# x1's transposes moved from TensorE to VectorE and DMA in a graph-attention kernel, with more rooms for u and the sums of x

## The chip, the cores and the metric

The kernel runs on one core of a Trainium2 chip. The core has a matrix engine (TensorE, PE in the profile; PEld is its weight load), VectorE (DVE), ScalarE (ACT), GpSimd (POOL), and SyncE (SP), which here only issues DMAs; 16 DMA engines move data between HBM and on-chip memory. Each engine works through its own instructions in the order in which the program gives them, and waits on semaphores for what it needs from others. The metric is the device time of one execution in microseconds, the median of several runs.

## The reference

There are 4096 nodes with 512 features each, and a matrix adj of 4096 x 4096. All is float32. Layer 0 is attention with adj as bias, then a residual and a layer norm; layer 1 is two graph convolutions, again with residual and norm:

```python
# layer 0
q = x @ Wq.T + bq;  k = x @ Wk.T + bk;  v = x @ Wv.T + bv
a = q @ k.T / sqrt(512) + adj + adj
x1 = layernorm(x + softmax(a, axis=-1) @ v)
# layer 1
h = relu(adj @ (x1 @ W1) + b1)          # W1: 512 x 128
out = layernorm(x1 + adj @ (h @ W2) + b2)
```

## The kernel before

**Groups and passes.** The 4096 query rows are cut into 8 groups of 512 (g = 0 to 7), and each group into 4 row tiles of 128 (r = 0 to 3). Scores are formed transposed: keys on the partitions, queries along the free dimension. q and k are never made. M = Wq.T Wk is formed first, and u = M.T xT for each group (half scale, plus a bias); the scores of group g are then xT.T u_g + adj.T. A pass over a group is 16 units of 7 gaps, 112 gaps, and each gap holds two score products of 256 columns. Softmax divides at the end: the maximum over keys is kept in macc, exp is taken by ACT, the row sums are kept in lacc, and p = x.T s is accumulated (so that v = x Wv.T is applied once per group, to p, by `rows_out_fast` or `rows_out`).

**Winograd's form of Strassen.** Most products are of 2 x 2 blocks with seven products in place of eight. A step k in ORDER = (1, 2, 6, 7, 5, 4, 3) multiplies one operand of the left side by one of the right side; operands are quarters (such as B11, B21, B22, B12) or sums of quarters (S1 to S4 on the left, T1 to T4 on the right). Its results accumulate in two PSUM banks, X and Y, that are read out after each step by DVE or ACT, so the bank must have been read before the step after next can use it. Each float32 product shows in the profile as two matmul records; a transpose by PE shows as one.

**What a gap holds besides scores.** A list `work` gives each stretch of units items with an estimated PE time, which are dealt out evenly among its gaps: in the pass of group g these are the 224 px items of group g - 1 (0.43 us each by the kernel's own estimate, `PX_US`), with the row items of group g - 2 put between them by `row_items`; `w(n)` stands for the next n px items. In the last pass, that of the px items of group 7, there are no scores, and w(n) is 3n items. px is done in phases: block of key pairs by step k. Phase n starts by asking for the x tile of phase n + 3 (`load_x`). `hooks`, filled by `at(unit, place, f)`, tell at which gap loads, sums and softmax steps are issued.

**First pass.** In the pass of group 0 there is no px yet. Its items are u of the later groups: u of groups 0 and 1 by `u_products` (16 products of 512 columns; group 0 before the first score), u of groups 2 to 7 by `u_fast` (28 products of 256 columns). u goes to HBM (`store_u`, POOL's queue) and is loaded again as the right operand of its group (`load_operand`). In the same pass x is loaded in pairs of tiles (`sum_x(q)`, into one of three rooms in t_sb, which is otherwise empty until x1's product with W1), read by DVE for a constant (`row_parts`), summed by POOL and stored as the left operands of px (xs_d). The left operands S1 to S4 of the scores are formed by DVE and stored too (`form_s`, `store_s`), and xT is loaded in two rotating tiles (`load_xts`).

**Rows.** `rows_out_fast` (groups 0 to 5, named by FAST_V) multiplies p by Wv in seven steps and adds the rest in XR; `rows_out` (groups 6 and 7) does it in 16 products of 512. Then, for each of the four row tiles, the norm is applied by ACT (`rows_norm`), PE transposes the tile in four 128 x 128 blocks into PSUM and ACT copies it out (`project`, lines 736 to 743), PE multiplies by W1 (`project2`, into t_sb), and POOL adds b2 and stores x1 for the last residual (`add_b2`). The order is in the list of `row_items`: the norms of row tiles 2, 3, 0 and 1 are followed within a few px items by their transposes. XR has one room (pool `rows`), so the rows of group g + 1 can be loaded only when those of g are done with. The same pool has one room with the tag "x1t", for a transposed tile and for the sum s3 of `rows_out_fast`.

**After attention.** The graph convolutions follow (`strassen`, lines 1041 and 1342), with the rows of group 7 among their first products. They are not touched.

Of the kernel before, what the change touches and what calls it, by code (L numbers as in the profile page):

```python
# [18 lines left out]
P = 128  # L19
# [5 lines left out]
def tile_graph_attention_then_gcn(  # L25
# [80 lines left out]
    c_d = [dram.tile([1, W], F32, name=f"c_d{g}") for g in range(NG)]  # L106
    u_d = [dram.tile([P, 7, 2, HW], F32, name=f"u_d{g}") for g in range(NG)]
# [46 lines left out]
    FAST_V = range(NG - 2)  # L154
# [10 lines left out]
    def new_uo(b, what):  # L165

        u = UO.setdefault(b, {})
        if what in (B11, B12):
            u[what] = uop.tile([P, 2, HW], F32, tag="b1", name=f"b1_{b}_{what}", bufs=3)
        else:  # L170
            u["all"] = uop.tile([P, 5, 2, HW], F32, tag="ut", name=f"uo{b}")
            u.update({k: u["all"][:, k - 1] for k in range(1, 6)})

    def store_u(b, what):
        if what in (B11, T4):
            nc.gpsimd.dma_start(u_d[b][:, what], UO[b][what])
        else:
            nc.gpsimd.dma_start(u_d[b][:, 1:6], UO[b]["all"])

    def m_sums():  # L180
# [6 lines left out]
        for out_, a, b_ in ((T1, T3, B11), (T2, B22, T1), (T4, B21, T2)):  # L187
            nc.gpsimd.tensor_tensor(MV[out_], MV[a], MV[b_], ALU.subtract)

    def m_t3():  # L190

        nc.vector.tensor_tensor(MV[T3], MV[B22], MV[T3], ALU.subtract)

    def u_fast(b):
# [4 lines left out]
        def read(k):  # L199
            ps = X["X" if k in (1, 6, 5, 3) else "Y"].rearrange("p (o i) -> p o i", o=2)  # L200
            if k == 1:
                new_uo(b, B11)
            if k == 6:
                new_uo(b, B12)
            if k == 7:
                new_uo(b, "all")
# [10 lines left out]
            if k == 4:  # L217
                for out_, a, b_ in ((T1, B12, B11), (T2, B22, T1), (T3, B22, B12)):
                    nc.gpsimd.tensor_tensor(u[out_], u[a], u[b_], ALU.subtract)
                store_u(b, B11)  # L220
            if k == 3:
                store_u(b, "all")
                owing.append(lambda: last(b))

        def last(b):
            nc.vector.tensor_tensor(UO[b][T4], UO[b][B21], UO[b][T2], ALU.subtract)
            store_u(b, T4)
# [25 lines left out]

    def u_products(b):

        ps = {}

        def one(o, c):
            def go():
                if c == 0:  # L260
                    ps[o] = bank("o", f"psu{b}_{o}", 4)
                nc.tensor.matmul(  # L262
                    ps[o], m_t[:, c, ts(o, P)], XTS[b][:, c, :], start=c == 0, stop=c == ND - 1
                )
                if c == ND - 1:
                    if o == 0:
                        if b:
                            for what in (B11, B12, "all"):
                                new_uo(b, what)
                        else:  # L270
                            for k in ORDER:
                                new_operand(0, k)
                    pair = (B11, B12) if o < 2 else (B21, B22)
                    for h in range(2):
                        nc.scalar.activation(
                            (UO[b][pair[h]] if b else UT[0, pair[h]])[:, o % 2, :],
                            ps[o][:, ts(h, HW)],
                            AF.Identity,
                            bias=ub_t[:, o : o + 1],
                            scale=HALF_SCALE,  # L280
                        )
                    if o == ND - 1:
                        if b:
                            combine_u(nc.gpsimd, UO[b])
                            for what in (B11, "all", T4):
                                store_u(b, what)
                        else:
                            combine_u(nc.vector, {k: UT[0, k] for k in range(7)})

            return go  # L290

        return [one(o, c) for o in range(ND) for c in range(ND)]

    def combine_u(eng, ut):
        for out_, a, b_ in ((T1, B12, B11), (T2, B22, T1), (T3, B22, B12), (T4, B21, T2)):
            eng.tensor_tensor(ut[out_], ut[a], ut[b_], ALU.subtract)
# [52 lines left out]
    def sum_x(q):  # L349

        w = t_sb[:, ts(q % 3, 8), :].rearrange("p (a b) c -> p a (b c)", a=4)
# [307 lines left out]
    def rows_out_fast(g, k, j):  # L659
# [6 lines left out]

        def read(k):
# [22 lines left out]
        if (k, j) == (1, 0):  # L690
            read_px()
            T["s3"] = rowp.tile([P, 2, HW], F32, tag="x1t", name=f"s3_{g}")
            tt(T["s3"], a11, a21, ALU.subtract)
            tt(a21, a21, a22, ALU.add)
# [17 lines left out]
        if j == 0 and n:  # L712
            read(ORDER[n - 1])
            if k == 2:
                tt(a11, a21, a11, ALU.subtract)
            if k == 6:
                tt(a12, a12, a11, ALU.subtract)
# [18 lines left out]
    def project(g, r):  # L736
# [6 lines left out]
        T["x1t", g, r] = x1t  # L743

# [9 lines left out]
    def row_items(g, between):  # L754
# [21 lines left out]
        w = between  # L776
        if g in FAST_V:
            return [
                *(item(0.86, rows_out_fast, g, k, j) for k in ORDER for j in range(2)),
                *w(1), item(0, rows_last, g), *norm(2), *norm(3), *w(2), *pro(2), *w(2), *pro(3),  # L780
# [12 lines left out]
    with tc.tile_pool(name="wqk", bufs=1) as wp:  # L793
# [47 lines left out]
        for w_t, w_n, name, b_t, b_r in (  # L841
            (wq_t, wq_n, "bk", bk_t, bk_r), (wk_t, wk_n, "bq", bq_t, bq_r)
        ):
            in_every_row(name, b_t, b_r)
            for o in range(ND):
                ps = bank("o", f"psw{o}", 4)
                for c in range(ND):
# [23 lines left out]
    for f in first[:ND]:  # L871
        f()
# [524 lines left out]
```

## Time and profile before

| | |
|---|---|
| median of three runs | 2306.16 us (2304.3 to 2306.61) |
| the profiled execution | 2308.84 us, span 2307.1 us |
| TensorE busy | 2276.3 us, 99% |
| VectorE busy | 1617.0 us, 70% |
| GpSimd busy | 1018.7 us, 44% |
| ScalarE busy | 399.8 us, 17% |
| DMA | 525.14 MB, mean 228 GB/s |

The span is the time from the first to the last instruction of the profiled execution; the 1.7 us between it and that execution's time lie around it. A line of the timeline reads: start, duration, engine, line of the kernel, operation, out<-in, tile shape, count, and in brackets the idle time before it with what ended it. A line of the waits reads: who waited, for whom, in total, how often, the longest. Busy time of matmuls includes a pipelined tail, so their price is read from start to start. Stages by time: M and u of group 0 until 39.5 us, the first pass until about 250, seven passes of 210 to 214 us (a group's rows begin at 442.13, 656.18, 870.58, 1084.5, 1298.95 and 1512.91 us), the pass without scores from 1718 to 1853, the graph convolutions to the end.

### The profile page before, as it was taken

The numbers are of one execution on the slowest core, as the hardware profiler recorded it, in microseconds if no ns is written. First come the engines' busy times: TensorE is split into PE (matmuls) and PEld (weight loads), VectorE is DVE, ScalarE is ACT, GpSimd is POOL, SyncE is SP. The second block draws the span as 40 slices with busy tenths as digits, with TensorE's granted clock in tenths as the row PEclk, the third lists the DMA queues.
The fourth block names the chain that finished last, engine by engine and source line by source line (L and its number), as shares of the span: only waits on it lengthen the run. The fifth ranks groups of instructions, "written<-read, shape, count | busy, mean of one in ns | idle before, by whom it ended". The sixth has DMA issues, their size and how long they took to land.

```text
span 2307.1 us, 28475 instructions
## 1 busy us (share of the span) xinstructions
PE 2276.3 (99%) x10672; PEld 1750.6 (76%) x10672; DVE 1617.0 (70%) x2276; ACT 399.8 (17%) x438; POOL 1018.7 (44%) x1009
## 2 busy tenths in 40 slices
PE   9999999999999999999999999999999999999998
PEld 5888788888888888888888888888876743333456
DVE  4676776687667756765776687568657877888864
ACT  2212211131122112111311121122102000000012
POOL 3565654185327424731653274237429830001043
PEclk9999999999999999999999999999999999999999
DMA  6999878667857684777578586947754468899996
GB/s 177 273 284 309 233 215 230 193 174 215 246 135 218 189 246 114 215 213 215 151 221 232 145 218 193 259 117 210 196 191 155 155 237 321 332 347 375 352 383 218
DMA packets 282711, 525.14 MB, mean 228 GB/s; under 512 B 23184, under 2 KB 130448, under 8 KB 281680
## 3 DMA queue, kind: packets, MB, share of 16 engines
q1 hardware_dynamic: 229040, 406.12, 52.3%
q0 software_dynamic: 43296, 105.39, 20.7%
q10 hardware_dynamic: 10240, 11.82, 1.7%
q8 instruction: 85, 1.39, 0.2%
q14 instruction: 50, 0.41, 0.0%
HBM read 475.27 MB, written 46.41 MB: 226 GB/s over the span
## 4 chain that ended last, share of the span: by engine, by line
PE 92%; DVE 4%; POOL 2%; DMA 1%; issue 1%; ACT 0%; SPq 0%; POOLq 0%; DVEq 0%; ACTq 0%
PE p L576 32%; PE X L436 18%; PE b L1041 15%; PE Y L436 14%; PE v L703 3%; PE acce L1342 2%; PE psu L234 2%; PE ops L1296 1%; PE tps L749 1%; PE psu L262 1%; PE x L651 1%; PE x1ps L740 1%; DVE s L449 1%; PE psm L856 1%; DMA u_d<-uo 1%
## 5 line engine op out<-in xcount | busy, mean ns | idle before, releaser
L576 PE MATMUL p<-s,xn 128*128 128x256 f32 x3584 | 895.6, 380 | 7.0 <-DVE s L531 2.6
L576 PEld LDWEIGHTS p<-s,xn 128*128 128x128 f32 x3584 | 677.1, 190 | 111.0 <-DVE s L531 5.6
L436 PE MATMUL X<-ut,sa 128*128 128x256 f32 x1984 | 513.4, 381 | 1.7 <-DVE s L449 1.7
L492 POOL TENSOR_TENSOR lacc<-lacc,s 128x512 f32<-128x512 f32 x240 | 344.1, 1434 | 203.2 <-ACT s L483 192.3
L436 PEld LDWEIGHTS X<-ut,sa 128*128 128x128 f32 x1984 | 370.1, 190 | 64.2 <-DVE s L449 15.3
L449 DVE TENSOR_TENSOR s<-X,s 128x512 f32<-128x512 f32 x256 | 176.3, 689 | 278.6 <-PE X L436 278.2
L436 PE MATMUL Y<-ut,sa 128*128 128x256 f32 x1408 | 361.6, 380 | 0.2 <-DVE s L449 0.2
L436 PEld LDWEIGHTS Y<-ut,sa 128*128 128x128 f32 x1408 | 266.8, 190 | 37.7 <-issue 1.4
L483 ACT ACTIVATE s<-s 128x1024 f32<-128x1024 f32 x128 | 135.3, 1057 | 790.3 <-DVE s L479 790.3
L458 DVE TENSOR_TENSOR macc<-macc,s 128x512 f32<-128x512 f32 x240 | 258.1, 1075 | 1.2
L449 DVE TENSOR_TENSOR s<-Y,s 128x512 f32<-128x512 f32 x192 | 131.9, 687 | 157.0 <-PE Y L436 155.7
L479 DVE TENSOR_TENSOR s<-s,mb 128x512 f32<-128x512 f32 x256 | 231.2, 913 | 2.4 <-ACT mb L399 2.4
L385 POOL DMA_DIRECT2D s<-in_adjT_dram x64 | 84.4, 1318 | 256.7 <-ACT s L380 255.9
L549 DVE TENSOR_TENSOR ot<-p,ot 128x512 f32<-128x512 f32 x248 | 168.9, 681 | 31.4 <-PE p L576 31.2
L1008 DVE TENSOR_TENSOR tt<-ck 128x1024 f32<-128x1024 f32 x112 | 138.4, 1270 | 38.7 <-PE b L1041 33.6
L1041 PE MATMUL b<-tt,st 128*64 128x512 f32 (+1 forms) x768 | 156.0, 541 | 0.0
L380 ACT COPY s<-cb 128x2048 f32<-128x2048 f32 x64 | 121.0, 1890 | 48.1 <-PE p L576 39.8
L519 POOL TENSOR_TENSOR s<-s 128x256 f32<-128x256 f32 x128 | 124.6, 974 | 0.6
L1041 PEld LDWEIGHTS b<-tt,st 128*64 128x64 f32 x768 | 53.9, 137 | 87.8 <-issue 79.9
L526 DVE TENSOR_TENSOR s<-s 128x512 f32<-128x512 f32 x128 | 114.3, 914 | 0.0
L520 POOL TENSOR_TENSOR s<-s 128x256 f32<-128x256 f32 x128 | 107.8, 842 | 10.0
L489 POOL TENSOR_TENSOR lacc<-s 128x512 f32<-128x512 f32 x8 | 10.6, 1321 | 197.9 <-ACT s L483 197.9
(186 smaller groups left out, 2112.6 us busy)
## 6 DMA issues: line engine op xcount, KB each, us to landing
ck<-in_adjT_dram SPq DMA_DIRECT2D x128, 1024.0 KB, 7.4
s<-in_adjT_dram POOLq DMA_DIRECT2D x64, 1024.0 KB, 11.5
sa<-s_d SPq DMA_DIRECT2D x224, 256.0 KB, 5.7
xn<-in_x_dram SPq DMA_DIRECT2D x192, 256.0 KB, 4.3
xn<-xs_d SPq DMA_DIRECT2D x96, 512.0 KB, 5.7
sa<-in_xT_dram SPq DMA_DIRECT2D x168, 256.0 KB, 4.7
xn<-xs_d SPq DMA_DIRECT2D x64, 256.0 KB, 3.9
ut<-u_d SPq DMA_DIRECT2D x49, 256.0 KB, 7.2
```

What stands on the lines that cost most here:

```text
L380: nc.scalar.copy(s, CB[g].unsqueeze(1).to_broadcast([P, 4, W]))
L436: nc.tensor.matmul(T["X" if k in (1, 6, 5, 3) else "Y"][:, ts(j, HW)], SA[g, d, a][:, c, j, :], UT[g, b][:, c, :], start=k in (1, 2, 7) an ...
L449: nc.vector.tensor_tensor(ck, ps, ck, ALU.add)
L458: nc.vector.tensor_tensor(MACC[g], MACC[g], ck[:, h, :], ALU.max)
L479: nc.vector.tensor_tensor(ck, ck, MB[g], ALU.subtract)
L483: nc.scalar.activation(ck, ck, AF.Exp, scale=2.0)
L492: nc.gpsimd.tensor_tensor(LACC[g], LACC[g], ck[:, h, :], ALU.add)
L519: nc.gpsimd.tensor_tensor(b12, b12, b11, ALU.subtract)
L549: nc.vector.tensor_tensor(to, ps, to, ALU.add)
L576: nc.tensor.matmul(T["PX" if k in (1, 6, 5, 3) else "PY"][:, ts(f, HW)], XN[n][:, q - a, ts(f, P)], quarters(g, q)[{1: 0, 2: 2, 6: 1, 7: 0 ...
L1008: nc.vector.tensor_tensor(t[:, :2], v[:, :, 1], v[:, 0], ALU.subtract)
L1041: nc.tensor.matmul(BK[n][k][ts(half, HH)], lhs, right(u, i, half, b), start=q == 0, stop=q == NP - 1,)
```

## The change

*x1's transposes.* For groups 0 to 5 the four row tiles are no longer transposed by PE. `turn_blocks` has DVE transpose a tile in blocks of 32 x 32 in one instruction, into the x1t tile. `store_blocks` has SP write it to HBM with four DMAs, one for each 32 partitions, in such places that the blocks come to lie transposed as well (runs of 32 words). `load_blocks` has SP load it back, over the row tile in XR, and `project2` multiplies from there. The list of `row_items` puts 70 px items after the last norm, then add_b2 of a tile, its transpose, its store 5 items later, the next tile's transpose and the load 16 items after the transpose, and the product 14 to 16 items after the load. Group 6 keeps PE's transposes, but its rows now go through `rows_out_fast`, with four of the sums on POOL instead of DVE.

*u.* `u_products` is gone: u of all groups comes from `u_fast`, which for group 0 writes into the operand tiles directly. M's sums for it are made before the first pass, and the products of M, the transposes of Wk and the constants are interleaved anew there. B21 gets a tile of its own and ACT's queue for its store, and the other tile (now four slices) is stored one step earlier. The work of the first pass starts at unit 1 in place of 0 and 3.

*Sums of x.* They have five rooms in place of three (two in the x tiles of px, which are idle then), and are loaded two units ahead in place of one. S1 to S4 are stored six gaps later.

```diff
-    FAST_V = range(NG - 2)
+    FAST_V = range(NG - 1)
...
-        if what in (B11, B12):
-            u[what] = uop.tile([P, 2, HW], F32, tag="b1", name=f"b1_{b}_{what}", bufs=3)
+        if what in (B11, B12, B21):
+            u[what] = uop.tile([P, 2, HW], F32, tag="b1", name=f"b1_{b}_{what}", bufs=4)
         else:
-            u["all"] = uop.tile([P, 5, 2, HW], F32, tag="ut", name=f"uo{b}")
+            u["all"] = uop.tile([P, 4, 2, HW], F32, tag="ut", name=f"uo{b}")
...
     def store_u(b, what):
-        if what in (B11, T4):
+        if what == B21:
+            nc.scalar.dma_start(u_d[b][:, what], UO[b][what])
+        elif what in (B11, T4):
             nc.gpsimd.dma_start(u_d[b][:, what], UO[b][what])
         else:
-            nc.gpsimd.dma_start(u_d[b][:, 1:6], UO[b]["all"])
+            nc.gpsimd.dma_start(u_d[b][:, 2:6], UO[b]["all"])
...
             if k == 4:
                 for out_, a, b_ in ((T1, B12, B11), (T2, B22, T1), (T3, B22, B12)):
-                    nc.gpsimd.tensor_tensor(u[out_], u[a], u[b_], ALU.subtract)
-                store_u(b, B11)
+                    (nc.gpsimd if b else nc.vector).tensor_tensor(
+                        u[out_], u[a], u[b_], ALU.subtract
+                    )
+                if b:
+                    store_u(b, B11)
+                    store_u(b, "all")
             if k == 3:
-                store_u(b, "all")
+                if b:
+                    store_u(b, B21)
                 owing.append(lambda: last(b))
...
-    def u_products(b):
...
     def sum_x(q):
 
-        w = t_sb[:, ts(q % 3, 8), :].rearrange("p (a b) c -> p a (b c)", a=4)
+        if q % 5 < 3:
+            w = t_sb[:, ts(q % 5, 8), :].rearrange("p (a b) c -> p a (b c)", a=4)
+        else:
+            w = xnp.tile([P, 4, 2 * P], F32, tag="xn", name=f"w{q}")
...
+        sum_ = (nc.gpsimd if g == NG - 2 else nc.vector).tensor_tensor
...
-            tt(T["s3"], a11, a21, ALU.subtract)
-            tt(a21, a21, a22, ALU.add)
+            sum_(T["s3"], a11, a21, ALU.subtract)
+            sum_(a21, a21, a22, ALU.add)
...
             if k == 2:
-                tt(a11, a21, a11, ALU.subtract)
+                sum_(a11, a21, a11, ALU.subtract)
             if k == 6:
-                tt(a12, a12, a11, ALU.subtract)
+                sum_(a12, a12, a11, ALU.subtract)
...
+    def turn_blocks(g, r):
+        T["x1t", g, r] = rowp.tile([P, ND, P], F32, tag="x1t", name=f"x1t{g}_{r}")
+        nc.vector.transpose(T["x1t", g, r].rearrange("p c i -> p (c i)"), XR[g][:, r, :])
+
+    def store_blocks(g, r):
+        x1t = T.pop(("x1t", g, r))
+        to = xt_d[g, r].rearrange("(b i) c (a j) -> a i c b j", i=32, j=32)
+        for a in range(4):
+            nc.sync.dma_start(
+                to[a], x1t[ts(a, 32)].rearrange("i c (b j) -> i c b j", j=32)
+            )
+
+    def load_blocks(g, r):
+        T["x1t", g, r] = XR[g][:, r, :].rearrange("p (c i) -> p c i", i=P)
+        nc.sync.dma_start(T["x1t", g, r], xt_d[g, r])
...
+        if g < NG - 2:
+            turn, store, load = (
+                lambda r, f=f: [item(0, f, g, r)] for f in (turn_blocks, store_blocks, load_blocks)
+            )
+            return [
+                *(item(0.86, rows_out_fast, g, k, j) for k in ORDER for j in range(2)),
+                *w(1), item(0, rows_last, g), *norm(2), *norm(3), *w(8), *norm(0), *w(2), *norm(1), *w(70),
+                *b2(2), *w(3), *turn(2), *w(5), *store(2), *b2(3), *w(11), *turn(3), *load(2), *w(5),
+                *store(3), *b2(0), *w(11), *turn(0), *load(3), *pro2(2), *w(5), *store(0), *b2(1),
+                *w(11), *turn(1), *load(0), *pro2(3), *w(5), *store(1), *w(11), *load(1), *pro2(0),
+                *w(14), *pro2(1),
+            ]
         if g in FAST_V:
...
-                *w(1), item(0, rows_last, g), *norm(2), *norm(3), *w(2), *pro(2), *w(2), *pro(3),
+                *w(1), item(0, rows_last, g), *norm(2), *norm(3), *w(2 + 2 * (g == NG - 2)), *pro(2), *w(2),
+                *pro(3),
...
-    work[0] = 3, [(0.86, f) for f in u_products(1)]
-    work[3] = 13, [(0.86, f) for g in range(2, NG) for f in u_fast(g)] + [(0, lambda: owing.pop()())] * 2
-    at(1, 0, m_sums)
-    at(3, 0, m_t3)
+    work[1] = 15, [(0.86, f) for g in range(1, NG) for f in u_fast(g)] + [(0, lambda: owing.pop()())] * 2
...
-        at(2 * d, 1, store_s, d)
+        at(2 * d + 1, 0, store_s, d)
     for q in range(NP):
-        at(max(q - 1, 0), 0, sum_x, q)
+        at(max(q - 2, 0), 0, sum_x, q)
```

## The prediction

> **What bounds the kernel now.** I read the page first, for busy time and the chain.
>
> ```profile
> span 2307.1 us, 28475 instructions
> ...
> PE 2276.3 (99%) x10672; PEld 1750.6 (76%) x10672; DVE 1617.0 (70%) x2276; ACT 399.8 (17%) x438; POOL 1018.7 (44%) x1009
> ...
> PE 92%; DVE 4%; POOL 2%; DMA 1%; issue 1%; ACT 0%; SPq 0%; POOLq 0%; DVEq 0%; ACTq 0%
> ```
>
> TensorE (PE) works 2276.3 of 2307.1 us: 31 us of idle in all. So time falls in two ways, by taking work from PE or by removing one of its few waits, and it rises wherever another engine is made late. The timeline of PE then gives the true price of a matmul, start to next start (busy times include a pipelined tail).
>
> ```profile
> 29.21 10.47 PE L262 MATMUL psu<-xt,m_t 128*128 128x512 f32 x24
> 39.52 1.03 PE L436 MATMUL X<-ut,xt 128*128 128x256 f32 x4
> ```
> ```profile
> 455.78 1.03 PE L703 MATMUL v<-wvs_t,ot 128*128 128x256 f32 x4
> 456.65 1.03 PE L436 MATMUL Y<-ut,sa 128*128 128x256 f32 x4
> ...
> 465.41 0.65 PE L740 MATMUL x1ps<-ident,xr 128*128 128x128 f32 x4 [0.40 <-ACT xr L639]
> ...
> 467.63 0.60 PE L740 MATMUL x1ps<-ident,xr 128*128 128x128 f32 x4
> 468.07 1.03 PE L436 MATMUL X<-ut,sa 128*128 128x256 f32 x4
> ```
>
> One 512-wide record takes 10.31 / 24 = 0.43 us (two records are one product), a 256-wide one 0.87 / 4 = 0.216, and the four transposes of a row tile 468.07 - 467.63 = 0.44. The third line also shows PE waiting 0.40 us for a norm. The waits of PE, whole run, name the rest:
>
> ```profile
> PE X L436 <- DVE s L449: 4.1, 5, 1.0
> ...
> PE x1ps L740 <- ACT xr L639: 2.3, 6, 0.4
> ...
> PE psu L234 <- ACT uo L211: 1.9, 1, 1.9
> ```
>
> The first and last fall between 40 and 260 us, the pass in which u and the sums of x are made. The waits of VectorE (DVE), ScalarE (ACT) and SyncE's queue (SP) in those 220 us say who is behind them; the windows show what the 1.9 us did to the clock (the last columns are PEclk, DMA share, GB/s).
>
> ```profile
> DVE t_sb L408 <- DMA t_sb<-in_x_dram: 9.7, 5, 5.0
> ```
> ```profile
> ACT uo L211 <- DMA u_d<-uo: 16.8, 3, 6.0
> ```
> ```profile
> SPq L353 <- DMA xs_d<-t_sb: 71.5, 9, 11.3
> ```
> ```profile
> 145.00:150.00 5.00, 5.00 (x17) 4.11 (x16) 2.55 (x5) 0.00 (x0) 0.95 (x1) 0.67 0.95 168
> ```
>
> Loads of x stand on SP until a room is stored; a u tile can't be written until its predecessor is stored.
>
> **The change part by part.**
>
> *1. Transposes leave PE.* 6 groups x 4 rows x 0.44 = **10.6 us** of PE, all on the bounding engine. The six waits of L740 for the norm (2.3 us) go too, since nothing on PE follows the norm until 70 items later: **2.3**. ACT loses 24 copies (L742) of 0.59 us; it is 17% busy, so that is worth nothing.
>
> *2. Seven half products for four whole ones.* u of groups 0 and 1 and the rows of group 6 go from 16 products of 512 (32 x 0.43 = 13.75) to 28 of 256 (56 x 0.216 = 12.1): 1.65 each. For u, **3.3**. For group 6 the stage (1718 to 1792 us) holds 7.5 us of PE waits, most of them on DVE and POOL: PE may arrive sooner and wait. DVE gets seven additions of 0.69 for four of 0.74 (+1.9 us); POOL gets four sums at 1.27 (+5.1), but idles 27 us just before 1724, and trades 12 small norm operations for 8. Between -3 and +3 us; I keep **1.6**, PE's own saving.
>
> *3. Rooms.* u: its slices other than B21 are stored one product earlier and B21 has its own tile, so ACT's 16.8 us of waiting and PE's 1.9 us should end, with the throttled clock behind it: 5 us at 0.67 is 1.7 us. Together 3.6. x: a sum's load stood at unit q-1 behind an xT load that waits for PE, so some were released 0.3 unit (3.5 us) before their use, against a landing of 8.1; at q-2, with five rooms, 1.3 units (15 us). Of DVE's 4.1 us brought onto PE I take 2. Against this, storing S is moved six gaps later, in three groups behind an xT load that PE releases, about 10 us before its room is wanted again; and the first adjacency load is now issued after a POOL sum, which waits on DVE, and has less time to land: after M's last product come an eviction and T2 on DVE (0.2 + 0.7 + 0.7), T4 on POOL (1.3) and the issue (1.3), 4.2 us, against 12.1 of u and 1.7 of scores until the first read, so 9.6 us where 11.5 is the median landing. I charge 1.6. Sum **4.0**, bounds -2 (both new waits, old ones stay) and +8.5 (all 6.8 of that pass and the clock). The prologue otherwise fills a 0.49 us wait for wk with other products: within that 1.6.
>
> On the clock the trace differs from the Trainium skill. "TensorE: Matmul & The Clock Gate", Part 1, has the clock halved after an idle window of about 3.4 us, so a 1.9 us wait would cost itself alone; the row shows 0.67 after it. By the page the sum would be 1.7 us smaller.
>
> *4. What is added.* Per row DVE transposes one 128x512 tile, SP issues four stores in runs of 128 bytes (2048 pieces) and one load of 256 KB, and PE multiplies from the loaded tile. No transpose or such store is in this trace.
>
> DVE: between 0.69 us (128x512 subtraction, L693) and 1.34 (the slowest such, L328), 24 times. In the stretch of the second px pass where they come:
>
> ```profile
> sum 52.00, PE 52.00 PEld 45.29 DVE 37.87 ACT 8.86 POOL 22.44; mean PE 13.00 PEld 11.32 DVE 9.47 ACT 2.22 POOL 5.61
> ```
>
> DVE is free 3.5 us of every 13, the spacing of the transposes: covered; without that cover it would be 17 to 32 us.
>
> The wait: the tile has one room, so transposes 2, 3 and 4 of a group stand on DVE until the stores before them have landed, with all score additions queued behind. A pass of 112 gaps takes 214 us, 1.9 per gap; 16 items of 0.43 (a gap takes 1.0) are 6.9 gaps, 13 us; the store comes 5 items, 4 us, after its transpose. That leaves **9 us**. Past that, the next score read may be one k-step (two gaps, 3.7 us) late before PE lacks a bank, so PE feels a landing over **12.7 us**. The nearest rows:
>
> ```profile
> x_d<-xb POOLq DMA_DIRECT2D x32, 256.0 KB, 4.0
> ...
> cb<-c_d ACTq DMA_DIRECT2D x7, 256.0 KB, 5.9
> ...
> c_d<-c_sb ACTq DMA_DIRECT2D x7, 2.0 KB, 9.8
> ```
> ```profile
> q10 hardware_dynamic: 528, 0.00, 0.5%
> ```
>
> Low: 4.0, the same bytes in 2 KB rows. High: c_d, 512 pieces, lands 3.9 us after cb; four times the pieces make 15.6, on 4.0: 20 us, 7 too many, 18 times, **130 us lost**. The last line (740 to 800 us, ACT's queue alone) gives 0.5% of 16 x 60 us for 528 packets, 9 ns each: the pieces hardly load the engines, so four DMAs side by side should take little longer than one. I take c_d's 9.8 and 1 us more, 11 us: DVE 2 us late, inside its cover. I charge **1.0** for coincidences with tight px steps.
>
> A page speaks against this. "VectorE: DVE Perf Modes", The three transpose paths, warns that a strided DMA copy as a transpose is 19 times slower than the crossbar (1309 ns per 128x128 block), when the innermost destination stride is large: estimated 25 us a block, 100 a row, and by that over 1500 us lost. Here the innermost run is 32 contiguous words, so I don't apply it. "DMA: Bandwidth & Descriptors", Specifications, puts line rate at 512 bytes and up; no row here shows 128.
>
> SP: the four issues take some 0.45 us each. The load stands 9 us after the stores, so SP stands 2 us at 11. Loads behind it: sa are issued 10 gaps (19 us) ahead and land in 5.7; xn three phases of 8 items (20 us) ahead, 5.7. Some 13 us are spare. The load itself has 13 us to its product, landing 4 to 6. POOL's adds of b2 and their stores are spread, none is added. ACT issues seven stores of B21, 0.4 us each, beside idle.
>
> **Sum.** 10.6 + 2.3 + 3.3 + 1.6 + 4.0 - 1.0 = 20.8. The profiled execution took 2308.84 us (span 2307.1 and 1.7 around it): 2288.0 after. It lies 2.7 above the median of the three runs, 2306.16, so I forecast **2286** for the median.
>
> **The rivals.**
>
> *A. The first pass and group 6 give nothing.* DMA share is about 1.0 from 150 to 250 us, so more rooms may only lengthen the queue. For: 317 to 320 GB/s there, with DMA share 0.99 to 1.02. Against: the 9.7 us of DVE are loads released late. Then 10.6 + 2.3 + 3.3 - 1 = 15 or, with the charges, 8: 2291 to 2300.
>
> *B. Slower: stores in pieces land late.* Place: second to fourth transposes of six groups, DVE waiting for x1t's room. For: c_d's 9.8 us for 2 KB. Against: its 9 ns packets. Price 18 x (landing - 12.7); it decides from 20.8 / 18 = 1.2, a landing near 14 us. At 15 us 2327, at 20 us 2416.
>
> *C. The saving becomes a wait of equal size*, PE for the loaded x1 or for xn behind it on SP: 24 x 0.8 us. For: SP is one queue. Against: 13 us spare. 2302 to 2311.
>
> **How the numbers follow.** Forecast 0.69 (own range 2274 to 2294: first pass +8.5 and group 6 +3 below, half of A above), A 0.13, B 0.14, C 0.04. 0.2% (4.6 us) is about what a measurement of this kernel can tell from no change. Faster: forecast and A, 0.82. Same: most of C, 0.03. Slower: B and the rest of C, 0.15. The range 2274 to 2304 leaves out B and most of C.
>
> **What would show it.** Right: no 128x128 transposes of xr in groups 0 to 5, passes 2 us shorter than 214, PE idle below 27 us, no wait of psu for uo, clock 1.00 at 140 us. Step 4: landing of xt_d under 12 us, and transpose durations near 0.7. Wrong: DVE waiting for DMA xt_d, PE X or p waiting for DVE in the middle of each pass, or SP standing at the load while PE waits for xn or sa.

## The result, and the profile after

The changed kernel takes 2309.37 us (median of 13 runs, 2306.82 to 2312.7) against 2304.51 for the kernel before in the same session (13 runs, 2304.09 to 2306.61). The ratio is 1.0021, with a 95% interval of 1.0014 to 1.0028: 0.2% slower, where 2286 and a gain were forecast. The profiled execution took 2311.35 us. That of the kernel before, 2308.84, lies 4.3 above its median, so the two traces differ by 2.5 us where the medians differ by 4.9.

The page of the changed kernel, span, busy time and the chain that ended last:

```profile
span 2309.6 us, 28654 instructions
...
PE 2266.9 (98%) x10648; PEld 1754.0 (76%) x10648; DVE 1624.2 (70%) x2311; ACT 389.1 (17%) x418; POOL 1011.8 (44%) x1007
...
PE 87%; DVE 8%; DMA 2%; issue 1%; POOL 1%; SPq 0%; ACT 0%; POOLq 0%; DVEq 0%
```

PE is busy 9.4 us less and idle 42.7 us where it was 30.8; DVE's share of the chain went from 4 to 8%. Work was taken off the bounding engine and came back as waits. (The forecast takes 15.5 us of work off PE. Busy time grows with the waits, too: e8 below has the same 10648 records, fewer waits and 2258.2 us.) The places where PE turns a group's maximum (`mt`) cut the span into stages in both traces. A runs to the second of these turns (group 1's) and holds the first pass and the pass of group 1, in which no rows are done; B runs from there to group 7's turn and holds the six passes with the rows of groups 0 to 5; C is the rest.

| us | A | B | C | span |
|---|---|---|---|---|
| before | 435.05 | 1280.47 | 591.58 | 2307.1 |
| changed | 429.99 | 1288.87 | 590.74 | 2309.6 |
| difference | -5.1 | +8.4 | -0.8 | +2.5 |

A gained, though not all it could: PE stood 9.4 us ahead at the first turn (227.98 us instead of 237.37) and had given back 4.3 of that by the second. B, where transposes and norm waits had been taken off PE, lost 8.4 us. The waits in the changed kernel's trace say for whom (who waited, for whom, total us, times, longest):

```profile
DVE x1t L727 <- DMA xt_d<-x1t: 33.2, 8, 4.8
...
PE p L552 <- DVE ot L525: 9.3, 8, 1.4
PE p L552 <- DVE s L507: 5.7, 10, 0.9
```

The first line is the wait that the forecast had named as its risk, and PE does not appear in it. The other two stand, for the most part, at the same two places of a pass, where the kernel before has no wait (its only one between 430 and 660 us is the 0.40 for a norm). In the timeline of PE, changed kernel:

```profile
472.53 0.70 PE L552 MATMUL p<-s,xn 128*128 128x256 f32 x2 [0.64 <-DVE s L507]
499.09 0.70 PE L552 MATMUL p<-s,xn 128*128 128x256 f32 x2 [1.43 <-DVE ot L525]
687.50 0.70 PE L552 MATMUL p<-s,xn 128*128 128x256 f32 x2 [0.64 <-DVE s L507]
714.07 0.70 PE L552 MATMUL p<-s,xn 128*128 128x256 f32 x2 [1.43 <-DVE ot L525]
```

These are px products waiting for DVE, 0.64 and 1.43 us in each of six passes, 57 and 31 us *ahead* of the first DVE transpose (529.69 us), before any of the new instructions. DVE at the second place:

```profile
494.08 0.68 DVE L525 TENSOR_TENSOR ot<-p,ot 128x512 f32<-128x512 f32 x1
494.68 0.41 DVE L507 TENSOR_TENSOR s<-s 128x256 f32<-128x256 f32 x1
495.01 1.75 DVE L455 TENSOR_TENSOR s<-s,mb 128x512 f32<-128x512 f32 x1
496.68 1.75 DVE L434 TENSOR_TENSOR macc<-macc,s 128x512 f32<-128x512 f32 x1
498.36 0.68 DVE L525 TENSOR_TENSOR ot<-p,ot 128x512 f32<-128x512 f32 x1
```

DVE runs without a gap here; PE takes its p bank at 499.09, when the read at 498.36 is done.

### The profile page after: what moved, and what is told of

Read it like the earlier page. It is cut to its first block, busy times and chain, and to the rows that moved or that the text cites. A ratio compares the mean times of both kernels' runs of the same rounds, so it can differ in the third digit from the quotient of the medians.

```text
span 2309.6 us, 28654 instructions
## 1 busy us (share of the span) xinstructions
PE 2266.9 (98%) x10648; PEld 1754.0 (76%) x10648; DVE 1624.2 (70%) x2311; ACT 389.1 (17%) x418; POOL 1011.8 (44%) x1007
## 4 chain that ended last, share of the span: by engine, by line
PE 87%; DVE 8%; DMA 2%; issue 1%; POOL 1%; SPq 0%; ACT 0%; POOLq 0%; DVEq 0%
PE p L552 28%; PE X L412 18%; PE b L1063 15%; PE Y L412 13%; PE psu L251 4%; PE v L681 3%; PE acce L1365 2%; DVE s L507 2%; DVE s L455 2%; DVE s L502 1%; DMA xt_d<-x1t 1%; PE tps L745 1%; PE ops L1319 1%; DVE s L425 1%; DVE ot L525 1%
## 5 line engine op out<-in xcount | busy, mean ns | idle before, releaser
L434 DVE TENSOR_TENSOR macc<-macc,s 128x512 f32<-128x512 f32 x240 | 236.6, 986 | 1.0
L455 DVE TENSOR_TENSOR s<-s,mb 128x512 f32<-128x512 f32 x256 | 221.9, 874 | 0.7 <-ACT mb L375 0.7
L525 DVE TENSOR_TENSOR ot<-p,ot 128x512 f32<-128x512 f32 x248 | 168.8, 681 | 24.9 <-PE p L552 24.7
L1030 DVE TENSOR_TENSOR tt<-ck 128x1024 f32<-128x1024 f32 x112 | 138.4, 1271 | 38.6 <-PE b L1063 33.2
L502 DVE TENSOR_TENSOR s<-s 128x512 f32<-128x512 f32 x128 | 130.5, 1036 | 0.0
L465 POOL TENSOR_TENSOR lacc<-s 128x512 f32<-128x512 f32 x8 | 10.6, 1323 | 201.3 <-ACT s L459 201.3
## 6 DMA issues: line engine op xcount, KB each, us to landing
s<-in_adjT_dram POOLq DMA_DIRECT2D x64, 1024.0 KB, 11.9
```

The source lines that it names most:

```text
L434: nc.vector.tensor_tensor(MACC[g], MACC[g], ck[:, h, :], ALU.max)
L455: nc.vector.tensor_tensor(ck, ck, MB[g], ALU.subtract)
L502: nc.vector.tensor_tensor(b, b, t2, ALU.subtract)
L525: nc.vector.tensor_tensor(to, ps, to, ALU.add)
L1030: nc.vector.tensor_tensor(t[:, :2], v[:, :, 1], v[:, 0], ALU.subtract)
```

## The experiments

The list of items gives each a charge and deals them evenly over a pass's 112 gaps. Before, four transposes (0.44) and four products (0.9) stood among the first 21 px items. Taken out or put 70 items later, 5.36 us of charge vanish there, at 1.0 us per gap, so every px step of the next 80 items comes 5 gaps earlier among the scores, while the softmax steps of DVE, placed by gap, do not move. Theory P (pace) says that this is what made PE wait. Theory S says it is the stores in pieces, for which DVE stands 33 us; F, that it is the first pass. In the diffs the changed kernel is the base unless said otherwise, and all ratios are to the kernel before.

**e1_paced: the old pace.**

```diff
+        def ghost(us):
+            return [(us, lambda: None)]
+        def late(r):
+            return [item(0, project2, g, r)]
...
-  *norm(2), *norm(3), *w(8), *norm(0), *w(2), *norm(1), *w(70),
+  *norm(2), *norm(3), *w(2), *ghost(0.44), *w(2), *ghost(0.44),
+  *w(3), *norm(0), *ghost(0.9), *w(2), *norm(1), *ghost(0.44), *w(2), *ghost(0.9), *w(2),
+  *ghost(0.44), *w(2), *ghost(0.9), *w(4), *ghost(0.9), *w(59),
...  # pro2(r) -> late(r) in the rest of the list
```

> The changed kernel with one difference: items that do no work, with the charges (0.44 and 0.9) that the four transposes and four products of x1 had before, stand at their old places in the list of a group's rows, and the late products are charged nothing. The px products then stand among the scores where they stood before the change (they stood 5 gaps earlier after it). Theory P (pace: the new stalls of PE on DVE come from px running 5 gaps earlier against DVE's softmax steps): the stalls of p on s L507 (0.64) and on ot L525 (1.43) in each of the passes of groups 1 to 7 go; a pass gains these 2.07 us and some 0.5 of restart, six passes 15 us: 2291 to 2297. If PE is only quicker than DVE whatever the order, part of it stays: 2297 to 2304. Theory S (DVE standing for the stores of x1 in pieces is what costs): order changes nothing, 2306 to 2313.

Measured: 2300.32 us (2296.02 to 2307.54), ratio 0.998 (0.9971 to 0.9988), above P's range and inside the one for "part of it stays". Stage B is 1274.43 us, 14.4 below the changed kernel's, but in a profiled execution that was the quickest of the twelve. Both waits are gone from all six passes; one of 0.81 to 1.00 us per pass, at 490.78 us in the first, came instead. P is supported in part, but the list has a second difference that I had not meant: its `w` add up to two fewer, so that x1's transposes and stores come two px items earlier, and DVE's wait for stores fell from 33 to 5.3 us. e5 takes that apart.

**e2_delayed: the same charge in one lump.**

```diff
-  *w(1), item(0, rows_last, g), *norm(2), ...
+  *ghost(5.36), *w(1), item(0, rows_last, g), *norm(2), ...
...  # pro2(r) -> late(r)
```

> As e1_paced, but the same charge (5.36 in all) is one empty item behind the rows' products and ahead of every px item, so that px starts 5 gaps later but nothing stands between its first steps. If lateness against DVE's steps is what counts, the time is that of e1_paced, 2291 to 2297. If what counted was that the row items stretched px's first block, in which a step has only four products, the wait of p on s L507 in the first block stays (0.64 and 0.27 of restart, six times, 5.4 us): 2296 to 2303. Theory S: 2306 to 2313.

Measured: 2348.2 us, ratio 1.0186 (1.0173 to 1.0199). None of the theories had this. The trace shows one wait of 5.07 to 6.40 us in five of the passes, PE X for DVE, at 559.49 us in the first, and behind it a slower clock (0.74 granted from 560 to 565 us); DVE there stands 8.21 us for a store of x1t whose four DMAs took 10.59 us of SP to issue, where the later groups of stores of these passes take 2.6 to 3.6. That is the forecast's rival B, at one place of each pass.

**e3_pe_turn: rows of groups 0 to 5 as before, all else changed.**

```diff
-        if g < NG - 2:
+        if False:
             turn, store, load = (
```

> The changed kernel with the rows of groups 0 to 5 as before the change (transposed by PE, products a few items later); u, the rooms and the rows of group 6 stay changed. By the two traces the passes with these rows lost 8.3 us against before, and the rest gained 6.2: 2298 to 2302. If the loss came from the first pass and its end (the rival F), this stays at 2306 to 2313.

Measured: 2303.13 us (2300.93 to 2304.65), ratio 0.9988 (0.998 to 0.9997), 1 us above the expected range; in the profiled run one load of xn (1.24 us, at 1154 us) accounts for that much. B is 1281.62, near before's 1280.47. So the loss is in the rows, and F falls.

**e4_spaced: transposes 24 items apart.**

```diff
-  *norm(1), *w(70),
+  *norm(1), *w(46),
...
-  *w(11), *turn(3), ...  *w(11), *turn(0), ...  *w(11), *turn(1), ...
+  *w(19), *turn(3), ...  *w(19), *turn(0), ...  *w(19), *turn(1), ...
```

> The changed kernel with the transposes by DVE 24 px items apart in place of 16, the first of them 24 items earlier, the last at the old place: a store has 15 us in place of 9 until the next transpose. DVE's waits for the store of x1t (33 us in all) should fall below 5. Theory P: the stalls that cost most lie 40 to 60 us ahead of the first transpose and stay; only the few later ones (0.6 each at 764, 980, 1411 and 1419 us) may go: 2304 to 2311. Theory S: DVE's 33 us were the loss, 2290 to 2300.

Measured: 2312.3 us, ratio 1.003 (1.0018 to 1.0042), 1 above P's range. DVE no longer waits for a store at all, and nothing is gained: the waits of 0.64 and 1.43 stand, and a new one of 0.6 (PE X for DVE, 529.49 us) comes in each pass where the first transpose now lies. S as the cause of the changed kernel's loss falls: taking the whole 33 us off DVE gave no time.

**e5, e6 and e7: the place of the stores.** All three move the transposes, stores and loads by two px items.

```diff
# e5_paced_late, on e1_paced:
-  *w(4), *ghost(0.9), *w(59),
+  *w(4), *ghost(0.9), *w(61),
# e6_delayed_early, on e2_delayed; e7_store_early, on the changed kernel:
-  *norm(1), *w(70),
+  *norm(1), *w(68),
```

> As e1_paced, with x1's transposes, stores and loads two px items later, where the changed kernel has them: each store is then issued one item behind a load of x for px on SP's queue, where e1_paced had it one item ahead of that load. Theory P (pace alone made e1 quick): as e1_paced, 2298 to 2303, DVE's wait for the store near 5 us. Theory Q (the place of the store on SP's queue was the gain of e1): DVE waits 30 us or more for xt_d again, and the time is at least 2305; if the wait comes to lie on PE as in e2_delayed, near 2345.

> As e2_delayed, with x1's transposes, stores and loads two px items earlier, which puts each store ahead of the load of x. e2_delayed lost 43 us, most of it where PE stood 5 to 6 us for a score read by DVE, which stood for the store. Theory Q: that wait goes and the time falls to that of e1_paced or up to 5 more (the px steps in the first block are closer): 2298 to 2306. If it is the empty item that did it, it stays at 2335 to 2350.

> The changed kernel with one difference: x1's transposes, stores and loads two px items earlier, ahead of the load of x on SP's queue. Theory P: DVE's wait for the store falls from 33 us to under 10, the few waits of PE behind the transposes may go (up to 4 us), the stalls of p on s L507 and ot L525 ahead of them stay: 2304 to 2309. Theory Q: most of what e1_paced gained, 2299 to 2303.

Measured: e5 2344.91 us (1.017, 1.0157 to 1.0184); e6 2307.3 (1.0008, 0.9999 to 1.0017), a little over its range; e7 2338.94 (1.0145, 1.0132 to 1.0159), outside both of its ranges: I had expected the store ahead of the load of x to be the better place in every case. Two px items later cost 45 us with the old pace (e1 to e5) and 41 with the lump (e6 to e2), and *saved* 30 with the new pace (e7 to the changed kernel). What is common to the slow ones (e2, e5, e7) shows in e5's timeline, SP, DVE and PE:

```profile
537.30 10.14 SPq L733 DMA_DIRECT2D xt_d<-x1t  x4
```
```profile
553.86 0.71 DVE L727 STREAM_TRANSPOSE x1t<-xr 128x512 f32<-128x512 f32 x1 [8.84 <-DMA xt_d<-x1t]
```
```profile
557.00 2.07 PE L412 MATMUL X<-ut,sa 128*128 128x256 f32 x4 [5.70 <-DVE s L425]
```

The four stores take 10.14 us to issue and have landed 16.6 us after the first was issued (553.86 - 537.30). DVE stands 8.84 us with the score reads behind it, PE 5.70, and then multiplies at half speed: four records, two products, in 2.07 us where they take 1.13 behind a shorter wait. The windows (last columns PEclk, DMA share, GB/s) show the granted clock:

```profile
550.00:555.00 5.00, 1.30 (x7) 0.79 (x5) 1.14 (x2) 0.00 (x0) 0.00 (x0) 0.87 1.09 297
555.00:560.00 5.00, 3.00 (x7) 2.47 (x8) 3.10 (x5) 1.06 (x1) 3.54 (x3) 0.50 0.95 259
```

Stage B of e5 is 1318.66 us, 44.2 above e1's. This stall stands in five of the six passes. In the sixth, the rows of group 5, PE waits 0.98 us at that place (1660.73 us); e13 and e14 show what differs there.

**e8_paced_spaced: e1 and e4 together.**

```diff
# on e1_paced
-  *w(4), *ghost(0.9), *w(59),
+  *w(4), *ghost(0.9), *w(35),
...  # *w(11), *turn(r) -> *w(19), *turn(r), as in e4
```

> e1_paced and e4_spaced together: the old pace of px, and the transposes 24 items apart, the last where e1_paced has it. DVE should not wait for a store at all, and no run should be caught by a late one: e1's runs went from 2296 to 2307, this one from 2295 to 2300, median 2296 to 2300. If the spread of e1's runs had another cause it stays as wide, median 2300.

Measured: 2295.87 us (2294.76 to 2297.69), ratio 0.9957 (0.9945 to 0.997). With the stores out of the way in both, pace alone is e4 against e8: 2312.3 - 2295.87 = 16.4 us. In that are e4's new waits of 0.6 at the first transpose, 3.8 in six passes, which neither e8 nor the changed kernel has. B is 1271.59, 8.9 below before and 10.0 below e3, which has PE's transposes: moved with the pace kept, they do give time. e1's spread has gone too.

**e9 and e11: the end of the first pass.** In the changed kernel PE waits four times there (timeline of PE):

```profile
226.89 1.30 PE L412 MATMUL X<-ut,sa 128*128 128x256 f32 x4 [2.20 <-DVE macc L434]
...
234.19 1.97 PE L412 MATMUL X<-ut,sa 128*128 128x256 f32 x8 [1.05 <-DVE s L425]
237.50 1.96 PE L412 MATMUL Y<-ut,sa 128*128 128x256 f32 x8 [1.35 <-DVE s L455]
...
241.98 1.13 PE L412 MATMUL X<-ut,sa 128*128 128x256 f32 x4 [0.78 <-DVE s L425]
```

DVE had read the score that the first of these needs 1.9 us earlier (224.28 + 0.68). What came last was the S operand. SP asked for it at 209.42 us, behind the last four stores of S (205.00 us). The DMA view of that one load, KB and us to landing, first in the changed kernel, then for the same load before (asked for at 217.59 us), where the stores stood further ahead:

```profile
sa<-s_d SPq DMA_DIRECT2D x1, 256.0 KB, 17.4
```
```profile
sa<-s_d SPq DMA_DIRECT2D x1, 256.0 KB, 11.4
```

209.42 + 17.4 is 226.8, the time at which PE goes on.

```diff
# e9_s_stores, on e8_paced_spaced
-        at(2 * d + 1, 0, store_s, d)
+        at(2 * d, 1, store_s, d)
# e11_u_longer, on e8_paced_spaced
-    work[1] = 15, [(0.86, f) ...
+    work[1] = 16, [(0.86, f) ...
```

> e8_paced_spaced with the stores of S1 to S4 six gaps earlier, where they were before the change. In e8 PE still waits 6.3 us between 227 and 243 us, at the first steps of the second pass, as in the changed kernel; the S operands of that pass were asked for 12 to 15 us ahead, behind the last four stores of S. If these stores make the loads late (they landed in 13 us, before the change in 8), the waits shrink to some 2 us and the time falls by 3 to 5, to 2291 to 2293. If it is the first pass being 9 us quicker against the same DMA traffic, nothing changes: 2295 to 2297.

> e8_paced_spaced with the u products of the first pass spread over 16 units in place of 15, so that some stand beside the first steps of the second pass, where PE waits 6.3 us. If loads are what PE waits for, the products fill the wait and the time falls by 3 to 5: 2291 to 2293. If the products keep rooms of S and make the loads later still: 2296 to 2302.

Measured: e9 2289.35 us (2288.15 to 2290.06), ratio 0.9927 (0.9914 to 0.9939); e11 2290.09, 0.9933 (0.992 to 0.9945). Both gained more than expected, some 6 us. In e9 three waits of 0.33 to 0.78 are left there; the two longer ones (timeline of PE):

```profile
226.65 0.66 PE L439 MATMUL mt<-ident,macc 128*128 128x128 f32 x4 [0.77 <-DVE macc L434]
...
236.31 0.92 PE L412 MATMUL X<-ut,sa 128*128 128x256 f32 x3 [0.78 <-DVE s L425]
```

Stage A is 424.35 us, 6.1 below e8's 430.44. The last stores of S, issued at 185 instead of 206 us, no longer stand ahead of the next pass's first operands: the same load lands in 10.3 us.

**e10_more_pace.**

```diff
# on e8_paced_spaced
-  *w(4), *ghost(0.9), *w(35),
+  *w(4), *ghost(0.9), *w(4), *ghost(0.5), *w(4), *ghost(0.5), *w(4), *ghost(0.5), *w(4),
+  *ghost(0.5), *w(19),
```

> e8_paced_spaced with four more empty items of 0.5 behind the 20th px item, four items apart. In e8 one wait of p per pass is left (0.92 to 1.03 us, at 492 us in the first), where DVE's read of ot comes late behind shifts that take 2.15 us each. If px is still too early there, the wait goes, 1.2 us a pass with the restart, 7 in all: 2288 to 2291. If DVE is full in that stretch whatever the pace, the wait moves: 2294 to 2298.

Measured: 2303.91 us, ratio 0.9993 (0.9984 to 1.0002), 8 us worse than e8 and worse than either expectation. The wait of 0.95 went; one of 1.07 to 1.30 on s L507 (499.76 us) and two of 0.35 and 0.32 on score reads came per pass. Px can be too late as well as too early, and this pace is no remedy for the wait that is left. In e8 DVE at that wait shows what fills it, POOL beside it:

```profile
484.90 4.31 DVE L455 TENSOR_TENSOR s<-s,mb 128x512 f32<-128x512 f32 x2
...
489.73 0.68 DVE L455 TENSOR_TENSOR s<-s,mb 128x512 f32<-128x512 f32 x1
```
```profile
485.19 3.47 POOL L468 TENSOR_TENSOR lacc<-lacc,s 128x512 f32<-128x512 f32 x2
488.63 1.18 POOL L495 TENSOR_TENSOR s<-s 128x256 f32<-128x256 f32 x1
```

The same subtraction takes 2.15 us each while POOL adds to lacc, and 0.68 a moment later. The Trainium skill, "SBUF — State Buffer", Who interferes with whom, has that a DVE instruction with two operands in SBUF contends with GpSimd instructions that read there; these rows agree, with a factor of 3.

**e12_act_queue: another queue.**

```diff
# on e5_paced_late
-            nc.sync.dma_start(
+            nc.scalar.dma_start(
                 to[a], x1t[ts(a, 32)].rearrange("i c (b j) -> i c b j", j=32)
```

> e5_paced_late (2345) with one difference: the stores of x1 in pieces are issued by ACT's queue, not SP's. In e5 the first four stores of a group took SP 10.1 us to issue, right behind a load of x, and 2.7 us elsewhere, and DVE stood 8.8 us for them. If that place on SP's queue is the cause, ACT issues them in about 2.7 us, DVE's wait for xt_d falls from 57 us to under 15, and the time to 2296 to 2306. If the DMA engines take that long for the pieces beside the loads, whatever the queue, ACT stands as long and exp with it: 2340 or more.

Measured: 2347.09 us, ratio 1.0172 (1.0158 to 1.0186), no better than e5 (2344.91). ACT took 12.83 us to issue the first four. SP's queue is not the cause. The Trainium skill, "DMA: Bandwidth & Descriptors", Issuing engines are not separate DMA queues, says that DMAs of all issuing engines end on the same 16 DMA engines; this run agrees, with 12.83 us on ACT's queue against 10.14 on SP's.

**e13 and e14: the store of c.** Each pass but the last stores 2 KB of constants, `c_d`, in 512 pieces of 4 bytes, issued at 538.26 us in the kernel before. In the DMA view of before, 530 to 555 us in 40 slices (busy share in tenths, GB/s), hardly anything moves for some 7 us behind it:

```profile
DMA  9988999940003987981000003001210699999999
GB/s 347 364 316 203 295 342 351 403 138 0 0 0 52 210 164 290 367 178 1 0 0 0 0 13 92 0 0 7 41 26 7 72 225 193 297 321 241 249 256 261
```

That alone could be a stretch with nothing to move. In the changed kernel, same window, the store of c is issued at 535.42 and the engines are busy, but slow:

```profile
DMA  2000279799999939799979525488999999999999
GB/s 75 5 0 0 15 272 226 229 400 255 197 173 325 118 11 48 16 39 23 34 39 82 57 49 16 74 166 285 382 338 215 210 272 249 265 308 285 298 318 246
```

In e2, e5 and e12 the stores that took 10 us and more were issued 7 us behind the store of c; in e7, 9 us; in e10, where four took 14.14, 6 us. The traces hold a comparison without any edit, too: the pass with the rows of group 5 has no store of c. In the changed kernel the second four stores take 7.52 to 8.48 us to issue in the five passes that have one, and 3.56 in the sixth; DVE stands in front of two transposes in each of the five, 3.4 to 4.8 us each time, and never in the sixth. In e5 the first four take 10.1 to 10.8 us in the five, 7.24 in the sixth.

```diff
# e13_c_store, on e5_paced_late; e14_c_store_alone, on the changed kernel
-            at(s0 - 8, 1, add_c0, g)
-            at(s0 - 8, 3, store_c, g)
+            at(s0 - (8 if g == 1 else 11), 1, add_c0, g)
+            at(s0 - (8 if g == 1 else 11), 3, store_c, g)
```

> e5_paced_late (2345) with one difference: the 2 KB store of c (512 pieces of 4 bytes, ACT's queue) and the addition ahead of it stand 21 gaps, some 40 us, earlier in the passes of groups 1 to 6. In the kernel before already, the DMA engines moved 0 to 50 GB/s for some 8 us behind that store; in e5, e2 and e12 the first store of x1t was issued 7 us behind it and took 10 to 13 us. Theory R (the store of c makes the stores of x1t late): DVE's wait for xt_d falls from 57 us to under 12, PE's 5.7 us per pass go, 2296 to 2304. If the pieces of x1t themselves are slow at that place: 2335 to 2350.

> The changed kernel with the store of c 21 gaps earlier and nothing else. Theory R: DVE's 33 us of waiting for xt_d fall below 12. Theory P: the waits of p on DVE 40 and 66 us into each pass's rows (0.64, 1.43) stay, so that the time hardly moves, 2304 to 2312; the store of c now falls into that stretch, and loads of xn may be late by it.

Measured: e13 2315.94 us, ratio 1.0041 (1.0028 to 1.0053), between its two ranges: 29 of e5's 45 us went, not all. Its first stores still take 7.70 us to issue, right behind the loads of x, and DVE's waits add up to 33.9. So c's store and something at that place, perhaps the loads, both hold the pieces up. e14 2301.73 us, ratio 0.9984 (0.9975 to 0.9993): 7.6 below the changed kernel. DVE's wait falls as R has it, and the time lies below P's range. Waits and the SP queue of e14:

```profile
DVE x1t L727 <- DMA xt_d<-x1t: 2.0, 2, 1.2
```
```profile
532.67 3.01 SPq L733 DMA_DIRECT2D xt_d<-x1t  x4
546.34 3.33 SPq L733 DMA_DIRECT2D xt_d<-x1t  x4
560.33 2.65 SPq L733 DMA_DIRECT2D xt_d<-x1t  x4
```

and the same queue in the changed kernel:

```profile
532.84 2.95 SPq L733 DMA_DIRECT2D xt_d<-x1t  x4
547.52 8.36 SPq L733 DMA_DIRECT2D xt_d<-x1t  x4
562.30 4.17 SPq L733 DMA_DIRECT2D xt_d<-x1t  x4
```

The second group shown stands for the others: 3.33 to 6.50 us in e14's five passes, 7.52 to 8.48 in the changed kernel's. The slow stretch goes with the store of c, now issued at 493.38 us. The DMA view of e14, 488 to 513 us:

```profile
DMA  9999999999999995290753566559999999996200
GB/s 170 193 200 203 203 213 223 242 320 380 400 337 346 307 89 3 13 25 5 56 87 62 59 66 52 72 184 356 395 429 369 354 392 377 388 383 234 80 26 2
```

PE waits 1.70 us for a load of x there (xn, 502.60 us), as the expectation had warned.

The wait of p on s L507 (0.64) stays in all six passes, as P has it. That on ot L525 (1.43) stays in only two of six, which is most of why e14 is quicker than P had it. What differs in the other four is whom POOL's additions slow. DVE and POOL of e14 in the fourth pass, and POOL of the changed kernel beside the DVE rows of 495.01 and 496.68 us above:

```profile
1138.93 0.68 DVE L455 TENSOR_TENSOR s<-s,mb 128x512 f32<-128x512 f32 x1
1139.53 0.68 DVE L434 TENSOR_TENSOR macc<-macc,s 128x512 f32<-128x512 f32 x1
1140.13 0.68 DVE L525 TENSOR_TENSOR ot<-p,ot 128x512 f32<-128x512 f32 x1
```
```profile
1138.64 4.54 POOL L468 TENSOR_TENSOR lacc<-lacc,s 128x512 f32<-128x512 f32 x2 [3.39 <-ACT s L459]
```
```profile
494.72 3.17 POOL L468 TENSOR_TENSOR lacc<-lacc,s 128x512 f32<-128x512 f32 x2 [3.26 <-ACT s L459]
```

In the four passes DVE's two steps take 0.68 us each and POOL's additions 2.27, in the two others and in the changed kernel DVE's take 1.75 and POOL's 1.6. DVE then reads ot 2.1 us later, and PE waits for it. So at the new pace the second wait comes only where DVE is slowed; what decides which engine is slowed, the traces do not show.

**e15 and e16: all together.**

```diff
# e15_both_ends, on e9_s_stores (e16_all: the edit of e13 as well)
-    work[1] = 15, [(0.86, f) ...
+    work[1] = 16, [(0.86, f) ...
```

> e9_s_stores with u's products over 16 units as in e11. Both took away the same waits of PE at the turn of the first pass (6 us in e8); in e9 0.8 and 0.8 us are left. If they are the same gain, 2288 to 2291; if e11 also hides the wait at the turn, 2287 to 2289.

> e15_both_ends with the store of c 21 gaps earlier. The transposes stand 24 items apart here and DVE waits for no store, so nothing is to gain there: 2287 to 2291. If the store of c makes loads of xn or the operands late in its new place, PE waits show 50 to 60 us into the pass and the time is 2292 or more.

Measured: e15 2290.4 us, ratio 0.9933 (0.9921 to 0.9946); e16 2291.47, 0.9937 (0.9924 to 0.9951). e16 lies 0.5 above its first range. e9's and e11's gains are the same gain, and where DVE waits for no store, moving c's store brings nothing. e9 remains the quickest: 2289.35 us, 0.73% below the kernel before and 20 below the changed one.

## Why the prediction was wrong

**Step 1, transposes leave PE, 10.6 + 2.3: this step failed.** PE's records fell as forecast and the waits for the norm went. But the step priced work taken off the bounding engine as time gained, 10.6 us, and no step asked what comes earlier when an item with a charge leaves a list that is dealt out evenly. Px came 5 gaps earlier against DVE's softmax steps, and PE waited 0.64 + 1.43 per pass, 12.4 us in six, and about 0.3 more at each restart. The 1.43 comes only where DVE's two steps are slowed beside POOL's additions (e14). Of 20.8 us of forecast gain this is the largest miss: 16.4 us between e4 and e8, which differ by the pace and two px items in the place of the transposes, and of which e4's own waits at the first transpose are some 4. Stage B should have fallen by 11.9 (12.9 less the charge of 1.0); it rose by 8.4, and with the old pace and spaced stores (e8) it fell by 8.9, with 5.7 us of one wait still in it.

**Step 4, the stores in pieces, charged at 1.0: the mechanism and landing were near, the price was too low.** The transpose takes 0.69 to 0.71 us, as forecast. Second group of stores, first issue to landing: 560.53 - 547.52 = 13.0 us where 11 was taken. DVE stood in front of ten transposes, 41.7 us in all (33.2 in the line of the list above, 8.5 in two waits that the list puts down to no engine), 2.3 per transpose where 2 was forecast. PE's waits behind that are three of 0.64 and one of 0.60 in the whole run, 2.5 us, and e14 has none of them; the rest of e14's 7.6 us is the wait on ot L525, 9.3 us in the changed kernel and 3.6 there, less 1.9 of new waits for loads of x. That the pieces hardly load the engines held: the trace's packet records give 49152 packets of 128 bytes 643 us together, 13 ns each where 9 was taken, 1.7% of 16 engines' span. What failed is the use of c_d's landing as a price for pieces alone. c_d is also a neighbour, issued in the same 20 us, and the stores are late in the five passes that have it.

**Rival B** (stores land late, 2327 to 2416, deciding near 14 us) was not the outcome, but it was two px items away: e2, e5 and e7, where the stores had landed 15.9, 16.6 and 13.7 us after the first issue, gave 2339 to 2348, and the changed kernel, with 13.0, cost PE 0.64 at most at such a place (764.25 us). The forecast gave it a place in all of the second to fourth transposes, 18 times. It comes once in each of five passes, and e5's 44.2 us above e1 are some 8.8 for each, with the clock and a second wait of some 1 us.

**Step 2, u: about right; step 3, rooms: partly.** The first score product starts at 38.26 us instead of 39.52, and the waits of DVE for x and of PE for u's tile are gone; A could gain 10.7 us (e9), more than the 3.3 and 4.0 forecast. The move of S's stores by six gaps, for which with the other new waits 1.6 was charged, cost 6.1 (e8 to e9), so that A gave 5.1. The forecast had watched the room that the stores keep, not the loads that they stand among.

**Group 6's rows, 1.6:** C gained 0.8. The forecast read most of the 7.5 us of PE's waits in that stage as waits on DVE and POOL; the list has 4.9 on DVE, 2.2 on ACT, 0.4 on DMA and none on POOL.

**The range.** Its lower end, 2274, takes the full bounds 8.5 and 3 off 2286, which already holds 4.0 and 1.6 of them; by these bounds it is 2280.

**Rival C** (the saving becomes a wait of equal size) had the right outcome, 2302 to 2311, with the wrong wait: not SP or the loaded x1, but px for DVE. That its range was hit is luck; its chance was put at 0.04.

What stays open: what decides in e14 whether DVE or POOL is slowed; the wait of 0.95 per pass that is left in e9; and what holds the stores in e13, which is still 16 us slower than e1 (PE waits 15.3 us for score reads there and 4.2 for loads of x). That the loads of x hold them was argued from their place, not tested. A second room for x1t was not tried.

## What to carry to other kernels

Where a list paces work by charges, taking an item out moves everything behind it: compare where the next steps come against the engines that feed them, and leave an empty charge in the old place until the rest has been moved too. An engine that waits for a transfer within its slack can be one small shift from costing a stall in every pass, so look at what else is issued in the same 20 us, above all small scattered stores, and leave room for it (e8: 24 items in place of 16) instead of meeting the mean. A store that nobody waits for still stands in front of loads that are waited for.

## What the runs showed of the hardware

- Behind a 2 KB store in 4-byte pieces the DMA engines moved 11 to 82 GB/s for 7 us, in most of which they were 0.7 busy or more (changed kernel); with that store 40 us earlier, the stretch moved with it (e14, 3 to 87 GB/s). Four stores of x1t, 64 KB each in 128-byte pieces, took 7.52 to 8.48 us to issue 12 us behind it, 3.56 in the pass without it (changed kernel). Right behind loads of x four took 7.24 us without it (e5, sixth pass).
- Where PE goes on after a wait of 5.70 us, its granted clock is 0.50 in the 5 us window (e5); after one of 1.91 us it is 0.67 in the next window (kernel before).
- A 128x512 subtraction on DVE with both operands in SBUF takes 0.68 us in most places. Beside POOL's additions to lacc either DVE is slowed, to 1.75 us (changed kernel) or 2.15 (e8), or POOL is, from 1.27 us an addition to 2.27 (e14). A DVE block transpose of 128x512 in float32 takes 0.70.
